# Layer 1 of a four-layer graph network in blocks of two chunks, with nine weight buffers, and three smaller edits in layer 3

## The chip, the cores and the metric

The kernel runs on one core of one Trainium2 chip. A core has five engines with a stream of instructions each: TensorE (PE in the profile; its weight loads are a row of their own, PEld), VectorE (DVE), ScalarE (ACT), GpSimd (POOL) and SyncE (SP), which issues most of the DMAs. The metric is the device time in microseconds (us) of one execution, given as the median of several runs. Lower is better.

## The reference, cut to what matters

Four layers, each of which ends in a residual sum and a layer norm. `x` is 2708 x 256, `adj` is 2708 x 2708, about 1.2% of it filled, with a full diagonal; all is float32.

```python
def layer1(x, adj, W, a, gamma, beta):          # attention with 4 heads of 64
    h = (x @ W).reshape(n, heads, head_dim)
    src = einsum('nhd,d->nh', h, a[:head_dim, 0])
    dst = einsum('nhd,d->nh', h, a[head_dim:, 0])
    e = src[:, :, None] + dst.T[None, :, :]
    e = where(e > 0, e, 0.2 * e)
    e = where(adj[:, None, :] > 0, e, -9e15)
    out = einsum('nhm,mhd->nhd', softmax(e, axis=-1), h).reshape(n, 256)
    return layernorm(out) * gamma + beta

def layer3(x, adj, neigh_W, lin_W):
    h = adj @ (x @ neigh_W.T) / (adj.sum(axis=1, keepdims=True) + 1.0)
    return concatenate([x, h], axis=-1) @ lin_W.T

x = layernorm(x + adj @ (x * W0))
x = layernorm(x + layer1(x, adj, ...))
x = layernorm(x + layer2(x, adj, ...))          # three heads of attention, two GRU cells
x = layernorm(x + layer3(x, adj, ...))
```

## The kernel before

**Tiles.** The 2708 rows make NT = 22 tiles of 128 rows (P), the last of 20. A tile of source rows is a "chunk" (c) where it is summed over. The four layers follow one another, with work of neighbouring layers drawn into one another where buffers allow. Each engine works through its own instructions in the order in which the program issued them, except that `tc.issue_after(instruction)` holds what stands under it until after that instruction in the order.

**Layer 1 (L780 to L858).** The destination rows are split into six groups of tiles (`spans`: 4, 4, 4, 4, 3, 3), worked in three pairs g = 0, 2, 4 of 1024, 1024 and 660 columns. Each pair takes two passes, q = 0 and 1, of two heads each: six passes over 22 chunks. The exponential of the leaky logits is split into factors that depend on one side only: `rise` belongs to the source row, `fall` to the destination. For each chunk and head of the pass DVE writes one tile p, 128 x 1024 (or 660), as max(fall, rise) x mask (L831, from a pool of five such tiles), where the fall tile `fall_b` holds the destination's factors in every partition. PE then does two things with the chunk's two p tiles. `heads` (L810 to L816) multiplies them with the 64 columns of `h` of each head into `acc`: four matmuls with weights 128x64 and 512 columns (330 in the last pair). `totals` (L818 to L825) sums them into `den`: four matmuls with weights 128x32. Both accumulate over all 22 chunks in PSUM (four buffers, tag `acc`), and ACT copies them out after the pass (L844, L852). The order is turned round with each chunk, T0 H0, H1 T1, T2 H2, H3 T3 and so on, if T and H are a chunk's totals and heads:

```python
for part in (heads, totals)[:: -1 if c % 2 == 0 else 1]:
    part(c, ps, dict(start=(c == 0), stop=(c == NT - 1)))
    if part is (totals, heads)[c % 2]:
        step(c)
```

`step(c)` issues one step of the work left over from the pair before: `layer1_end` (transposes L688 and L689, normalisation on ACT, DVE and POOL) in pass q = 0, `layer1_logits` (L750, L767) in pass q = 1.

**Fall tiles.** `fall_b` is [128, 4 heads, 1024], 16 KB in each partition, in two buffers. `load_fall` (L412) fills half of one by a DMA that gives one DRAM row to all partitions (`bcast_rows`, L106). The tiles of g = 0 and g = 2 are loaded on GpSimd's queue in layer 0, after its tiles 3, 7, 11 and 15; that of g = 4 on SP's queue at the start of the third pair (L784 to L786), once the first buffer is free.

**Layer 3.** `adj @ h` is done by seven products in place of eight: the destination columns come in three units of 430, 430 and 366 columns (`units3`), each over MH = 11 chunks. `seven` (L307) makes four sums of blocks on DVE (L313 to L316, out of the tile `p` that SP's queue loads, L273) and issues seven matmuls (L326). `gathered` (L330) adds the accumulators up at a unit's end (L337, L340, L343, L344); it returns its last add, and every chunk of the next unit, whichever it is, is issued with its sums behind it: `with tc.issue_after(summed.ins): seven(...)` (L1410). The first unit's sums stand behind the last gathering of layer 2, and in this unit the last steps of layer 2's node update (L1163 to L1233) are drawn in between the matmuls.

`rows3` and `row3` (L1365 to L1390) finish 128 rows at a time: PE transposes, DVE adds the residual (L1368), takes the moments (`bn_stats` L170, `bn_aggr` L172, an add L174), GpSimd takes the power -1/2 (L175). The row tile is closed by `flush()`, which is called after the next row tile's moments: DVE forms -mean x rs (L1361), ACT applies scale and bias (L1362), and a DMA stores the tile (L1363), on ACT's queue for odd tiles and on SP's for even ones. Two row tiles, 19 and 20 (`last3`), are not part of the units; they are summed directly at the end (L1428), with the rows of the last unit drawn in between, and tile 20 is the last to be closed.

Of the kernel before, what the change touches and what calls it, by code (L numbers as in the profile page):

```python
# [9 lines left out]
F32 = mybir.dt.float32  # L10
# [4 lines left out]
AF = mybir.ActivationFunctionType  # L15
ALU = mybir.AluOpType
# [3 lines left out]
P = 128  # L20
# [7 lines left out]
def kernel(  # L28
# [24 lines left out]
    nc = tc.nc  # L53
    N, F = x.shape
    NT = -(-N // P)
    FC = F // P
    HD = a1.shape[0] // 2
    H = F // HD
# [3 lines left out]
    W = GT * P  # L62
# [7 lines left out]
    spans = [(sum(sizes[:i]), sum(sizes[: i + 1])) for i in range(len(sizes))]  # L70
# [11 lines left out]
    last3 = [t for t in range(NT) if min(P, N - t * P) == P][-2:]  # L82
# [22 lines left out]

    def bcast_rows(d, lo, n):  # L106

        return bass.AP(tensor=d.tensor, offset=d.offset + lo, ap=[[0, P], [d.shape[1], d.shape[0]], [1, n]])

# [32 lines left out]
    fall_d = dram.tile([H, N], F32, name="fall_d")  # L142
# [249 lines left out]
    mask = mask_pool.tile([P, NT, MP], FP8, name="mask")  # L392
# [5 lines left out]
    if True:  # L398
# [6 lines left out]
        rise = keep.tile([P, NT, H], F32, name="rise")  # L405
# [5 lines left out]
        if True:  # L411
            def load_fall(dst, g, queue):  # L412
                at, w = spans[g][0] * P, width(*spans[g])
                off = at - spans[g - g % 2][0] * P
                queue.dma_start(dst[:, :, off : off + w], bcast_rows(fall_d, at, w))

            def layer1_projection(pool, t):
                n = sz(t)
# [23 lines left out]

                for g in [g for g, (lo, hi) in enumerate(spans[:4]) if hi == t + 1]:
                    load_fall(falls[g // 2], g, nc.gpsimd)

# [4 lines left out]
            with pool("l0", 2) as l0:  # L450
# [165 lines left out]
                fallp = fall_stack.enter_context(pool("fallp", 2, side="right"))  # L616
                falls = [fallp.tile([P, H, 2 * W], F32, tag="fall_b", name="fall_b") for _ in range(2)]
                nc.sync.dma_start(gamma_b, bcast(gamma, F))
# [36 lines left out]
            if True:  # L655
# [124 lines left out]
                for g in range(0, len(spans), 2):  # L780
                    segs = spans[g : g + 2]
                    at, w = segs[0][0] * P, width(segs[0][0], segs[-1][1])
                    if g >= 4:
                        falls.append(fallp.tile([P, H, 2 * W], F32, tag="fall_b", name="fall_b"))  # L784
                        for i in range(len(segs)):
                            load_fall(falls[-1], g + i, nc.sync)  # L786
                    cols = [(lo * P - at, width(lo, hi)) for lo, hi in segs]
# [18 lines left out]
                    for q in range(H // 2):  # L806
# [19 lines left out]

                        for c in range(NT):
                            ps = []
                            for i in range(2):
                                p = l1.tile([P, 2 * W], F32, tag="p", name="p", bufs=5)  # L830
                                nc.vector.scalar_tensor_tensor(  # L831
                                    p[:, :w], falls[g // 2][:, 2 * q + i, :w], rise[:, c, 2 * q + i : 2 * q + i + 1],
                                    mask[:, c, at : at + w], ALU.max, ALU.mult,
                                )
                                ps.append(p)

                            for part in (heads, totals)[:: -1 if c % 2 == 0 else 1]:
                                part(c, ps, dict(start=(c == 0), stop=(c == NT - 1)))
                                if part is (totals, heads)[c % 2]:
                                    step(c)  # L840
                        got = []
# [263 lines left out]
    with (  # L1105
# [250 lines left out]
        def flush():  # L1356

            while ended:
                t, o, mean, rs = ended.pop()
                n = sz(t)  # L1360
                nc.vector.scalar_tensor_tensor(mean, mean, -1.0, rs, ALU.mult, ALU.mult)  # L1361
                nc.scalar.activation(o[:n], o[:n], AF.Identity, scale=rs, bias=mean)  # L1362
                (nc.scalar if t % 2 else nc.sync).dma_start(out[t * P : t * P + n, :], o[:n])  # L1363
# [31 lines left out]
        for u, (_, w) in enumerate(units3):  # L1395
            m = accumulators()
            for i, c in enumerate(lead):
                early3 = u == 0 and max(ends_at[2 * c], ends_at[2 * c + 1]) + 1 < len(units)
                if u == 0:
                    if not early3:  # L1400
                        while urgent or later:
                            between()
                    hq[c] = quarter_sums(xqp, h3, c, "hq")
                pa = nright.tile([P, 2, 2, W], F32, tag="p", name="p", bufs=3)
                load_pairs(units3, u, c, pa, NH3, tiles3)
                if i == MH - 3:
                    o8 = hold.tile([P, 4 * W // F, F], F32, tag="blk", name="o8", bufs=2)
                    for j, t in enumerate(complete(u)):
                        nc.gpsimd.dma_start(o8[: sz(t), j], y3_d[t])
                with tc.issue_after(summed.ins):  # L1410
                    seven(nright, m, pa, h3, hq[c], c, w, i == 0, i == MH - 1, range(7) if early3 else (2, 5))
            y, summed = gathered(nleft, m, w, W, "yk")
            later.append(rows3(u, y, o8))
# [287 lines left out]
```

## Time and profile before

| | us |
|---|---|
| median of three runs | 1857.94 |
| the runs | 1857.53, 1857.94, 1859.26 |
| the profiled execution | 1858.13 |
| its span, first to last instruction | 1856.3 |
| PE busy in it | 1826.3 |
| DVE busy | 1279.9 |
| ACT busy | 700.2 |
| POOL busy | 272.3 |
| p tiles on DVE (L831), 264 of them | 293.8 busy, 30.0 idle before them |
| heads on PE (L813), 1056 records | 214.5 busy |
| totals on PE (L822), 1056 records | 114.9 busy |
| -mean x rs on DVE in layer 3 (L1361), 22 of them | 3.5 busy, 10.7 idle before them |

A row of the profile's groups names the line, the engine, the operation and the tiles (output <- inputs), how often it ran, how long it was busy, and how long its engine stood idle just before it, with what ended that idle time. In a timeline the first number is the start in us from the span's start and the second the length; x16 says that sixteen such records follow one another. An f32 matmul leaves two records. In a windows table each line is a stretch of time with the busy time and number of instructions (x) of each engine in it. The granted TensorE clock was 0.998 of full speed.

### The profile page before, as it was taken

The numbers are of one execution on the slowest core, as the hardware profiler recorded it, in microseconds if no ns is written. First come the engines' busy times: TensorE is split into PE (matmuls) and PEld (weight loads), VectorE is DVE, ScalarE is ACT, GpSimd is POOL, SyncE is SP. The second block draws the span as 40 slices with busy tenths as digits, with TensorE's granted clock in tenths as the row PEclk, the third lists the DMA queues.
The fourth block names the chain that finished last, engine by engine and source line by source line (L and its number), as shares of the span: only waits on it lengthen the run. The fifth ranks groups of instructions, "written<-read, shape, count | busy, mean of one in ns | idle before, by whom it ended". The sixth has DMA issues, their size and how long they took to land.

```text
span 1856.3 us, 23052 instructions
## 1 busy us (share of the span) xinstructions
PE 1826.3 (98%) x7512; PEld 1031.6 (56%) x7512; DVE 1279.9 (69%) x2263; ACT 700.2 (38%) x1444; POOL 272.3 (15%) x426
## 2 busy tenths in 40 slices
PE   9999999999999999999999999999999999999997
PEld 7788842233345886788444444444445556654555
DVE  5443479999898654654558887777887768844664
ACT  3544410023144203211555665555665546321011
POOL 1211220001012411000002000111200302111111
PEclk9999999999999999999999999999999999999999
DMA  8344410100002667764556665454554535634764
GB/s 299 134 148 148 161 41 1 30 1 7 18 7 73 146 145 191 170 145 116 171 143 203 181 175 164 120 169 113 163 156 110 148 100 139 164 106 118 199 166 122
DMA packets 435101, 237.32 MB, mean 128 GB/s; under 512 B 184363, under 2 KB 422348, under 8 KB 432540
## 3 DMA queue, kind: packets, MB, share of 16 engines
q1 hardware_dynamic: 422414, 208.66, 41.2%
q0 software_dynamic: 8208, 22.59, 3.8%
q10 hardware_dynamic: 4350, 4.50, 0.7%
q8 instruction: 62, 1.02, 0.2%
q14 instruction: 67, 0.55, 0.1%
HBM read 223.00 MB, written 12.66 MB: 127 GB/s over the span
## 4 chain that ended last, share of the span: by engine, by line
PE 85%; DMA 5%; DVE 4%; SPq 3%; issue 1%; ACT 1%; POOL 1%; POOLq 0%; DVEq 0%; ACTq 0%
PE m L326 40%; PE acc L813 11%; PE acc L213 8%; PE bank L1187 7%; PE den L822 6%; PE bank L1163 3%; SPq L273 2%; PE bank L1230 2%; PE gate L1062 2%; DMA strip<-in_adj_t_dram 2%; DMA p<-in_adj_t_dram 1%; PE pm L423 1%; PE pq L983 1%; PE m L1428 1%; DMA blk<-in_adj_t_dram 1%
## 5 line engine op out<-in xcount | busy, mean ns | idle before, releaser
L831 DVE SCALAR_TENSOR_TENSOR p<-fall_b,rise,mask 128x1024 f32<-128x1024 f32 (+1 forms) x264 | 293.8, 1156 | 30.0 <-PE den L822 14.7
L1328 ACT ACTIVATE p<-st,e_neg 128x1024 f32<-128x1024 f32 (+1 forms) x198 | 197.4, 1040 | 195.0 <-PE m L326 189.2
L326 PE MATMUL m<-s,xq 128*128 128x512 f32 (+3 forms) x660 | 230.1, 467 | 0.0
L813 PE MATMUL acc<-p,h 128*64 128x512 f32 (+2 forms) x1056 | 214.5, 548 | 0.0
L326 PE MATMUL m<-p,xq 128*128 128x512 f32 (+1 forms) x396 | 182.9, 544 | 0.1
L213 PE MATMUL acc<-turn,strip 128*128 128x257 f32 x792 | 181.8, 379 | 0.0
L1331 ACT ACTIVATE p<-p 128x1024 f32<-128x1024 f32 (+1 forms) x198 | 178.8, 942 | 0.2
L313 DVE TENSOR_TENSOR s<-p 128x512 f32<-128x512 f32 (+3 forms) x132 | 81.7, 619 | 137.6 <-PE m L326 114.4
L326 PE MATMUL m<-p,x 128*128 128x512 f32 (+1 forms) x396 | 167.7, 542 | 0.3 <-DVE supt L343 0.3
L1332 DVE TENSOR_TENSOR p<-p,blk 128x1024 f32<-128x1024 f32 (+1 forms) x132 | 143.0, 1103 | 35.7 <-ACT p L1331 25.7
L326 PEld LDWEIGHTS m<-s,xq 128*128 128x128 f32 x660 | 124.5, 190 | 76.1 <-issue 59.5
L213 PEld LDWEIGHTS acc<-turn,strip 128*128 128x128 f32 x792 | 147.2, 190 | 20.3
L813 PEld LDWEIGHTS acc<-p,h 128*64 128x64 f32 x1056 | 69.9, 136 | 136.7 <-issue 128.0
L326 PE MATMUL m<-s,x 128*128 128x512 f32 (+3 forms) x330 | 127.2, 467 | 0.0
L326 PEld LDWEIGHTS m<-p,xq 128*128 128x128 f32 x396 | 74.6, 190 | 76.9 <-issue 61.1
L326 PEld LDWEIGHTS m<-p,x 128*128 128x128 f32 x396 | 74.8, 190 | 75.5 <-issue 60.7
L822 PE MATMUL den<-p,h 128*32 128x512 f32 (+2 forms) x1056 | 114.9, 548 | 0.0
L468 ACT ACTIVATE below<-strip 128x384 bf16<-128x384 f32 x132 | 78.5, 594 | 69.8 <-DMA strip<-in_adj_t_dram 66.4
L284 POOL TENSOR_TENSOR blk<-blk,offdiag 128x128 f32<-128x128 f32 (+3 forms) x50 | 30.9, 622 | 367.4 <-DMA blk<-in_adj_t_dram 300.0
L326 PEld LDWEIGHTS m<-s,x 128*128 128x128 f32 x330 | 62.0, 190 | 39.2 <-issue 34.3
L314 DVE TENSOR_TENSOR p<-p 128x512 f32<-128x512 f32 (+3 forms) x132 | 82.0, 621 | 2.3
L316 DVE TENSOR_TENSOR s<-p,s 128x512 f32<-128x512 f32 (+3 forms) x132 | 81.1, 615 | 1.9
(285 smaller groups left out, 2586.5 us busy)
## 6 DMA issues: line engine op xcount, KB each, us to landing
strip<-in_adj_t_dram SPq DMA_DIRECT2D x19, 1408.0 KB, 6.3
blk<-in_adj_t_dram SPq DMA_DIRECT2D x88, 256.0 KB, 3.4
blk<-in_adj_t_dram SPq DMA_DIRECT2D x88, 192.0 KB, 4.1
pa<-in_adj_t_dram SPq DMA_DIRECT2D x110, 128.0 KB, 2.6
turn<-in_adj_t_dram SPq DMA_DIRECT2D x44, 256.0 KB, 3.1
blk<-in_adj_t_dram SPq DMA_DIRECT2D x88, 128.0 KB, 2.5
p<-in_adj_t_dram SPq DMA_DIRECT2D x88, 128.0 KB, 2.7
turn<-in_adj_t_dram SPq DMA_DIRECT2D x44, 192.0 KB, 3.2
```

What stands on the lines that cost most here:

```text
L213: at = nc.tensor.matmul(acc, s[:, c, :n], rhs(c), start=(c == 0), stop=(c == NT - 1))
L313: nc.vector.tensor_tensor(s1, a21, a22, ALU.add)
L314: nc.vector.tensor_tensor(a21, a21, a11, ALU.subtract)
L316: nc.vector.tensor_tensor(s4, a12, s2, ALU.subtract)
L326: nc.tensor.matmul(dst[:, :w], lt, rt, start=start and not (one_bank and i in (3, 4, 6)), stop=stop and not (one_bank and i in (1, 2, 5)))
L813: nc.tensor.matmul(acc[s][i * HD : (i + 1) * HD, :ws], hs[c][:, 2 * q + i, :HD], ps[i][:, p0 : p0 + ws], **flags,)
L822: nc.tensor.matmul(den[j : j + CT, :ws], hs[c][:, 2 * q + i, HD + 1 - CT :], ps[i][:, p0 : p0 + ws], **flags,)
L831: nc.vector.scalar_tensor_tensor(p[:, :w], falls[g // 2][:, 2 * q + i, :w], rise[:, c, 2 * q + i : 2 * q + i + 1], mask[:, c, at : at + w] ...
L1187: nc.tensor.matmul(g[:, :w], lt, rt, start=(q == 0), stop=(q == len(terms) - 1))
L1328: nc.scalar.activation(p[:, :, :w], st_k[:, :, :w], AF.Relu, scale=-1.0, bias=e_neg[:, at, k : k + 1])
L1331: nc.scalar.activation(p[:, :, :w], p[:, :, :w], AF.Exp, scale=-1.0)
L1332: nc.vector.tensor_tensor(p[:, :, :w], p[:, :, :w], blk[:, i, :, :w], ALU.mult)
```

## The change

1. In layer 1 the chunks are taken in blocks of two. All four p tiles of a block are issued first, then one part for both chunks, then the other for both; the order of the parts is turned round with each block: T0 T1 H0 H1, H2 H3 T2 T3, T4 T5 H4 H5. The pool of p tiles has nine buffers instead of five (16 KB more in a partition). `step` is called once after each part.
2. A fall tile holds the two heads of one pass, [128, 2, 1024], in two buffers (16 KB less in a partition). The two of g = 0 are loaded on GpSimd's queue in layer 0, after its tiles 3 and 7, two DMAs each time; the other four on SP's queue, each after the p tiles of a pass of the pair before, two DMAs each.
3. In `flush()` -mean x rs is formed on GpSimd instead of DVE. For the very last tile (20) one DVE operation, (x - mean) x rs, stands in for both the product and ACT's activation.
4. The first chunk of each unit of layer 3 is not issued behind the gathering's last add.

PE's instructions are the same in kind and number. DVE has 22 small operations (128x1, one of them 20x1) less and one of 128x256 more, ACT one of 128x256 less, GpSimd 21 of 128x1 more.

```diff
@@ -103,9 +103,9 @@
                 yield t, a, b
             lo -= sz(t)
 
-    def bcast_rows(d, lo, n):
-
-        return bass.AP(tensor=d.tensor, offset=d.offset + lo, ap=[[0, P], [d.shape[1], d.shape[0]], [1, n]])
+    def bcast_rows(d, row, rows, lo, n):
+
+        return bass.AP(tensor=d.tensor, offset=d.offset + row * d.shape[1] + lo, ap=[[0, P], [d.shape[1], rows], [1, n]])
 
     def pool(name, bufs=1, **kw):
         return tc.tile_pool(name=name, bufs=bufs, reuse_waits="tile", **kw)
@@ -409,10 +409,10 @@
         ps_t = ps_t_stack.enter_context(pool("ps_t", 4, space=PSUM, side="right"))
         ps_acc = acc_stack.enter_context(pool("ps_acc", 4, space=PSUM))
         if True:
-            def load_fall(dst, g, queue):
+            def load_fall(dst, g, q, queue):
                 at, w = spans[g][0] * P, width(*spans[g])
                 off = at - spans[g - g % 2][0] * P
-                queue.dma_start(dst[:, :, off : off + w], bcast_rows(fall_d, at, w))
+                queue.dma_start(dst[:, :, off : off + w], bcast_rows(fall_d, 2 * q, 2, at, w))
 
             def layer1_projection(pool, t):
                 n = sz(t)
@@ -440,8 +440,9 @@
                 nc.scalar.copy(turned[:, :n], pf[:H, 0, :n])
                 nc.gpsimd.dma_start(fall_d[:, t * P : t * P + n], turned[:, :n])
 
-                for g in [g for g, (lo, hi) in enumerate(spans[:4]) if hi == t + 1]:
-                    load_fall(falls[g // 2], g, nc.gpsimd)
+                for g in [g for g, (lo, hi) in enumerate(spans[:2]) if hi == t + 1]:
+                    for q, dst in enumerate(falls):
+                        load_fall(dst, g, q, nc.gpsimd)
 
             w0_b = keep.tile([P, F], F32, name="w0_b")
             quarter = keep.tile([P, CT], F32, name="quarter")
@@ -614,7 +615,7 @@
                 gamma_b = keepr.tile([P, F], F32, name="gamma_b")
                 beta_b = keepr.tile([P, F], F32, name="beta_b")
                 fallp = fall_stack.enter_context(pool("fallp", 2, side="right"))
-                falls = [fallp.tile([P, H, 2 * W], F32, tag="fall_b", name="fall_b") for _ in range(2)]
+                falls = [fallp.tile([P, 2, 2 * W], F32, tag="fall_b", name="fall_b") for _ in range(H // 2)]
                 nc.sync.dma_start(gamma_b, bcast(gamma, F))
                 nc.sync.dma_start(beta_b, bcast(beta, F))
                 layer0_scale(ahead, last)
@@ -780,10 +781,6 @@
                 for g in range(0, len(spans), 2):
                     segs = spans[g : g + 2]
                     at, w = segs[0][0] * P, width(segs[0][0], segs[-1][1])
-                    if g >= 4:
-                        falls.append(fallp.tile([P, H, 2 * W], F32, tag="fall_b", name="fall_b"))
-                        for i in range(len(segs)):
-                            load_fall(falls[-1], g + i, nc.sync)
                     cols = [(lo * P - at, width(lo, hi)) for lo, hi in segs]
                     cut = min(cols[1][0], (w // 2 + P // 4) // (P // 2) * (P // 2))
                     halves_at = [(0, cut), (cut, w - cut)]
@@ -824,20 +821,28 @@
                                         ps[i][:, p0 : p0 + ws], **flags,
                                     )
 
-                        for c in range(NT):
-                            ps = []
-                            for i in range(2):
-                                p = l1.tile([P, 2 * W], F32, tag="p", name="p", bufs=5)
-                                nc.vector.scalar_tensor_tensor(
-                                    p[:, :w], falls[g // 2][:, 2 * q + i, :w], rise[:, c, 2 * q + i : 2 * q + i + 1],
-                                    mask[:, c, at : at + w], ALU.max, ALU.mult,
-                                )
-                                ps.append(p)
-
-                            for part in (heads, totals)[:: -1 if c % 2 == 0 else 1]:
-                                part(c, ps, dict(start=(c == 0), stop=(c == NT - 1)))
-                                if part is (totals, heads)[c % 2]:
-                                    step(c)
+                        fall_b = falls.pop(0)
+                        for b, c0 in enumerate(range(0, NT, 2)):
+                            block = {}
+                            for c in range(c0, min(c0 + 2, NT)):
+                                block[c] = []
+                                for i in range(2):
+                                    p = l1.tile([P, 2 * W], F32, tag="p", name="p", bufs=9)
+                                    nc.vector.scalar_tensor_tensor(
+                                        p[:, :w], fall_b[:, i, :w], rise[:, c, 2 * q + i : 2 * q + i + 1],
+                                        mask[:, c, at : at + w], ALU.max, ALU.mult,
+                                    )
+                                    block[c].append(p)
+
+                            for i, part in enumerate((heads, totals)[:: -1 if b % 2 == 0 else 1]):
+                                for c, ps in block.items():
+                                    part(c, ps, dict(start=(c == 0), stop=(c == NT - 1)))
+                                if c0 + i < NT:
+                                    step(c0 + i)
+                        if g + 2 < len(spans):
+                            falls.append(fallp.tile([P, 2, 2 * W], F32, tag="fall_b", name="fall_b"))
+                            for i in range(len(spans[g + 2 : g + 4])):
+                                load_fall(falls[-1], g + 2 + i, q, nc.sync)
                         got = []
                         for s, (p0, ws) in enumerate(cols):
                             sb = keepr.tile([P, W], F32, tag=f"sum{q}{s}", name=f"sum{q}{s}")
@@ -1358,8 +1363,11 @@
             while ended:
                 t, o, mean, rs = ended.pop()
                 n = sz(t)
-                nc.vector.scalar_tensor_tensor(mean, mean, -1.0, rs, ALU.mult, ALU.mult)
-                nc.scalar.activation(o[:n], o[:n], AF.Identity, scale=rs, bias=mean)
+                if t == last3[-1]:
+                    nc.vector.tensor_scalar(o[:n], o[:n], mean, rs, ALU.subtract, ALU.mult)
+                else:
+                    nc.gpsimd.tensor_scalar(mean, mean, rs, -1.0, ALU.mult, ALU.mult)
+                    nc.scalar.activation(o[:n], o[:n], AF.Identity, scale=rs, bias=mean)
                 (nc.scalar if t % 2 else nc.sync).dma_start(out[t * P : t * P + n, :], o[:n])
 
         def row3(t, o, acc):
@@ -1407,7 +1415,7 @@
                     o8 = hold.tile([P, 4 * W // F, F], F32, tag="blk", name="o8", bufs=2)
                     for j, t in enumerate(complete(u)):
                         nc.gpsimd.dma_start(o8[: sz(t), j], y3_d[t])
-                with tc.issue_after(summed.ins):
+                with tc.issue_after(summed.ins) if i else nullcontext():
                     seven(nright, m, pa, h3, hq[c], c, w, i == 0, i == MH - 1, range(7) if early3 else (2, 5))
             y, summed = gathered(nleft, m, w, W, "yk")
             later.append(rows3(u, y, o8))
```

More of the change, by code (lines that the diff above doesn't have):

```diff
@@ L1 @@
 import itertools
-from contextlib import ExitStack
+from contextlib import ExitStack, nullcontext
 import concourse.bass as bass
```

## The prediction

> **What bounds the kernel now.** I read the page's busy shares first, then the chain of waits, then each stage that the change touches: the six passes of layer 1 as windows, one pass as a timeline of PE and of DVE, and the timeline of the end of layer 3.
>
> ```profile
> PE 1826.3 (98%) x7512; PEld 1031.6 (56%) x7512; DVE 1279.9 (69%) x2263; ACT 700.2 (38%) x1444; POOL 272.3 (15%) x426
> PE 85%; DMA 5%; DVE 4%; SPq 3%; issue 1%; ACT 1%; POOL 1%; POOLq 0%; DVEq 0%; ACTq 0%
> ```
>
> PE is busy nearly always and holds 85% of the chain that ended last, so a gain must either shorten PE's own stream or remove one of the 30 us (1856.3 - 1826.3) in which PE does nothing. The windows below are the six passes of layer 1, in order.
>
> ```profile
> core 0: us, PE busy (x) PEld busy (x) DVE busy (x) ACT busy (x) POOL busy (x), PEclk, DMA share, GB/s
> 247.50:309.00 61.50, 61.50 (x366) 17.20 (x369) 57.05 (x55) 2.06 (x8) 8.21 (x6) 1.00 0.04 10
> 309.00:368.80 59.80, 59.80 (x360) 16.23 (x356) 54.57 (x44) 2.33 (x4) 0.00 (x0) 1.00 0.04 11
> 368.80:431.90 63.10, 63.10 (x384) 18.86 (x380) 60.68 (x85) 26.28 (x129) 8.44 (x7) 1.00 0.04 13
> 431.90:498.00 66.10, 66.10 (x408) 21.80 (x404) 53.88 (x48) 9.20 (x25) 6.34 (x9) 1.00 0.06 17
> 498.00:541.60 43.60, 43.60 (x388) 19.30 (x380) 41.64 (x76) 22.63 (x117) 5.91 (x5) 1.00 0.00 1
> 541.60:587.90 46.30, 46.30 (x401) 22.12 (x394) 38.82 (x60) 12.42 (x37) 11.03 (x20) 1.00 0.08 23
> ```
>
> PE's busy time equals the window in every pass: 340.4 us without a gap. DVE, which makes the p tiles, is busy 306.6 us and comes second, closest in passes 3 and 5 (60.7 of 63.1, 41.6 of 43.6). PE's timeline in pass 2:
>
> ```profile
> 318.93 1.92 PE L822 MATMUL den<-p,h 128*32 128x512 f32 x16
> 320.79 3.65 PE L813 MATMUL acc<-p,h 128*64 128x512 f32 x16
> 324.37 1.92 PE L822 MATMUL den<-p,h 128*32 128x512 f32 x16
> 326.23 3.65 PE L813 MATMUL acc<-p,h 128*64 128x512 f32 x16
> ```
>
> Two chunks' totals (T) start every 5.44 us. An f32 matmul leaves two records, heads (H, 64 columns) run two abreast and totals (32 columns) four abreast, so two chunks of H take 8 slots and two of T take 4. Weight loads inside one H stand 0.43 us apart (0.4285). Eight slots are 3.43 us, but H lasts 3.58 (324.37 - 320.79); four are 1.71, but T lasts 1.86. Each change between the two shapes thus costs 0.15 us. The check on all six passes: 12 x 0.4285 x 11 = 56.6 us for a pass of 1024 columns and 36.8 for one of 660, about 2.6 of transposes in passes 1, 3 and 5, some 5.2 of logits in passes 4 and 6, and the changes of shape counted in PE's order, 26, 22, 26, 30, 26, 30 = 160, give 61.8, 59.8, 63.0, 66.2, 43.3, 46.3: the measured lengths within 0.3 us. So nothing but PE's stream sets layer 1.
>
> The end of the kernel (timeline, all engines):
>
> ```profile
> 1839.97 4.48 PE L1428 MATMUL m<-turn,p 128*128 128x256 f32 x20
> ...
> 1844.60 0.16 DVE L1361 SCALAR_TENSOR_TENSOR bn_mv<-bn_mv,bn_rs 128x1 f32<-128x1 f32 x1 [0.72 <-POOL bn_rs L175]
> ...
> 1846.70 0.15 DVE L1361 SCALAR_TENSOR_TENSOR bn_mv<-bn_mv,bn_rs 20x1 f32<-20x1 f32 x1 [0.72 <-POOL bn_rs L175]
> 1846.78 0.47 DVE L1368 SCALAR_TENSOR_TENSOR y<-m,rdeg,y 128x256 f32<-128x256 f32 x1
> ...
> 1848.84 0.16 DVE L1361 SCALAR_TENSOR_TENSOR bn_mv<-bn_mv,bn_rs 128x1 f32<-128x1 f32 x1 [0.72 <-POOL bn_rs L175]
> 1849.03 0.60 ACT L1362 ACTIVATE y<-y,bn_mv,bn_rs 128x256 f32<-128x256 f32 x1 [1.54 <-DVE bn_mv L1361]
> 1849.65 0.33 SPq L1363 DMA_DIRECT2D out_dram<-y  x1
> ```
>
> PE's last matmul ends at 1844.45, yet its row starts on DVE at 1846.78. DVE stands 0.72 us before each L1361 for GpSimd's power (L175), a row takes it 2.15 us (start to start of L1368), and a backlog has built up.
>
> [...] 0.15 us a change, none between matmuls of one shape. [...] for 128x1 the trace's nearest row is L175, 0.54 us alone at the end, and I use that.
>
> **Part 1, blocks of two chunks.** T0 T1 | H0 H1 H2 H3 | T2 T3 T4 T5 | H4...: one change of shape per block instead of one per chunk. Counting changes in PE's new order, which is known without running it (first pass not quite regular, transposes included), gives 24, 12, 18, 22, 19, 22 = 117. 43 fewer x 0.149 us = -6.4 us. PE's instructions are the same.
>
> What this needs from DVE: four p's before each block, out of nine buffers instead of five. In pass 2 DVE makes a p each 1.24 us, 54.6 a pass; with the other vector work that its new order puts into each pass I get 60.5 us against a PE pass of 63.1 - 1.2 = 61.9 for pass 3, 41.4 against 43.6 - 1.0 = 42.6 for pass 5 and 42.2 against 46.3 - 1.2 = 45.1 for pass 6. It keeps up, but by about 1 us, with three p's of lead as the only store. Bounds: nothing, or up to 2 us of stalls over both passes. I take +0.4. At pass boundaries the denominators are done four matmul groups earlier, so their copies on ACT free the buffer that the next pass's first H needs within T0 T1 (1.86 us); at layer 1's end the 0.85 us of acc copies come after the last H, +0.15 to 0.3, inside the same allowance.
>
> **Part 2, fall tiles by half.** Four DMAs in layer 0 stay four on GpSimd's queue with half the bytes; the second and third pairs add eight on SP where two stood. They stand on SP between the loads of layer 0 and those of layer 2, whose first begins at 588; SP's issue of one takes 0.37 us and waits only for the last DVE read of the pass before. They land 5.6 to 7.1 us after issue in the trace and are read a whole pass (some 60 us) later. 0 us; they would cost only if landing took longer than a pass.
>
> **Part 3, mean times scale on GpSimd.** Per row DVE loses a 128x1 operation (0.16) and, above all, the wait: 0.47 + 0.43 + 0.18 + 0.15 with their gaps is 1.35 us, less than the 1.5 us in which PE delivers rows. The backlog goes, and the last row starts at about 1844.65: -2.13 us. For the last tile, one DVE operation of 128x256 (0.42, from the row of L170, up to 0.5) replaces 0.16 and 0.60 with their handover: 1848.84 to 1849.26 instead of 1849.63, -0.37. From SP's issue to the end the 6.65 us stay. Sum -2.5 (bounds -2.7 to -2.0). GpSimd gets 21 operations of about 0.55; its queue carries a power each 1.5 us at the end, so 1.1 of 1.5 is used, and the power of the last row stands ahead of nothing that is unfinished. The earlier rows' outputs leave later by half a us and are not last.
>
> **Part 4, first chunk's sums not behind the gathering.** Each unit of layer 3 starts with sums (L313 to L316) held behind the last add of the gathering (L344). For unit 0 PE stands 2.75 us between the two first chunk's stretches:
>
> ```profile
> 1609.99 0.60 DVE L313 TENSOR_TENSOR s<-p 128x430 f32<-128x430 f32 x1
> 1610.35 0.99 PE L326 MATMUL m<-p,turn 128*128 128x430 f32 x2 [1.03 <-DMA p<-in_adj_t_dram]
> 1613.78 0.99 PE L326 MATMUL m<-p,turn 128*128 128x430 f32 x2 [1.72 <-DMA p<-in_adj_t_dram]
> ```
>
> In the new order L313 to L315 stand before the gathering's first add (L337, 1606.88 now). Their data is issued from 1599.6 and lands at about 1606.6 to 1607, so the gathering ends about 2 us later (1.8 us of sums less the idle time before it), while PE has its sums sooner: I take 2.0 us of stall for 2.75. In units 1 and 2 the sums fit in DVE's idle time before the gathering (6.3 and 5.0 us) and stalls of 0.37 and 0.80 shrink by half. In all -0.75 - 0.2 = about -0.9, bounds -2.5 to +3.
>
> Sum: -6.4 + 0.4 - 2.5 - 0.9 = -9.4 us. The profiled execution, span 1856.3 and 1.8 around it, 1858.1 us, becomes 1848.7. It is 0.2 above the median of the runs (1857.94), so the forecast is 1848.6 us.
>
> **The rivals.**
> - B: DVE becomes the bound. For: passes 3 and 5 have 2 us to spare now, and PE wants to be faster by 1.2 each; a lead of two blocks must also be built up at each start. Against: DVE's waits in layer 1 (14.7 us behind totals, 13.8 behind heads) are all for PE. Layer 1 then gains 2.5 us: 1848.6 + 3.9 = 1852.5.
> - C: the data of the first chunk's sums comes too late in all units, the gathering waits behind them and PE with it, with no gain and 1.3 us of new stall at each of the three (2 us of delay, 0.7 of it covered by PE's next matmuls): 1848.6 + 0.9 + 3 x 1.3 = 1853.4. Against: SP has issued those loads 7 us before in unit 0.
> - D, the slower side: the matmuls of layer 3's unit 0 hide the node update of the last group of columns. In the new PE order two or three fewer of them stand before each half-step's transposes (L1220). From the last gate matmul (1681.00) to those transposes (1684.16) is 3.16 us, four times; each of seven tiles then waits 0.57 for its copy. All uncovered: 12.6 + 4.0 = 16.6 us, 1865.2. It decides from 13.1 us on, that is only when nearly all of it is uncovered; PE stands still for 0.6 us between 1615 and 1720 now.
> - E: the change of shape costs what it did, because the 0.15 belongs to each first matmul of a chunk and not to the change. Then only parts 3 and 4 are left: 1855. The pass check, with its transposes, speaks against it.
>
> **How the numbers follow.** Forecast 0.62, B 0.17, C 0.12, D 0.05, E 0.04. Bounds of the forecast's own costs: 1845.5 (stalls nothing, first chunk -2.5) to 1851.0. The range reaches to B and C and leaves out D and E: 1845.5 to 1853.5. About 0.2%, 3.7 us, can be told from no change: faster is below 1854.2, which the forecast, B and three quarters of C give, 0.88; within 0.2%, 0.07; slower, 0.05.
>
> **What would show it.** Passes of 61.2, 58.3, 61.9, 64.9, 42.6 and 45.1 us, each shorter than now by the changes of shape that it loses (2, 10, 8, 8, 7, 8) times 0.149; den and acc groups of 32 records; DVE's idle in them still for PE. At the end no wait of DVE for GpSimd but the last, and the last row starting 0.2 us after PE's last matmul. In unit 0 one stall of PE of about 2 us. The prediction fails if PE waits for p in layer 1, or if PE's stalls grow between 1600 and 1700.

## The result, and the profile after

The changed kernel takes 1853.53 us (median of seven runs, 1850.31 to 1855.39) beside 1859.17 (1857.53 to 1859.54) of the kernel before: a ratio of 0.9967, interval 0.9957 to 0.9976. On the base of the prediction that is 1857.94 x 0.9967 = 1851.8 us, inside the range of 1845.5 to 1853.5 and 3.2 us above the forecast of 1848.6; the bare median lies on the range's upper edge. Of the 9.4 us forecast, about two thirds came. The profiled execution took 1851.74 us with a span of 1850.0, 6.3 less than before. The page of the changed kernel, busy shares and the chain of waits:

```profile
PE 1821.8 (98%) x7512; PEld 1038.5 (56%) x7512; DVE 1273.9 (69%) x2242; ACT 699.1 (38%) x1443; POOL 273.0 (15%) x447
PE 91%; DMA 3%; DVE 2%; ACT 1%; SPq 1%; issue 1%; POOL 0%; POOLq 0%; DVEq 0%; ACTq 0%
```

PE is still the engine that counts. To see where the 6.3 us come from, I cut both spans, which are given to 0.1 us, at PE's own events:

| stretch | before | after | difference |
|---|---|---|---|
| start to layer 1's first totals | 247.49 | 246.77 | -0.7 |
| to layer 2's first matmul | 343.75 | 340.93 | -2.8 |
| to layer 3's first matmul | 1016.48 | 1016.32 | -0.2 |
| to PE's last matmul | 236.73 | 235.47 | -1.3 |
| to the end of the span | 11.85 | 10.51 | -1.3 |

The first row is no effect of the change: over the thirteen profiles of this study it lies anywhere between 246.8 and 252.8. So runs are compared below by these stretches. Layer 1 repeats to about 0.1 us; layer 3 doesn't: in the four kernels that leave part 4 out (before, and blocks, tail and split of the experiments) it takes 235.7 to 237.5 us. The six passes of layer 1 in the changed kernel, as windows:

```profile
core 0: us, PE busy (x) PEld busy (x) DVE busy (x) ACT busy (x) POOL busy (x), PEclk, DMA share, GB/s
246.80:308.70 61.90, 61.90 (x362) 17.56 (x361) 59.24 (x59) 2.64 (x9) 4.94 (x6) 1.00 0.09 26
308.70:367.10 58.40, 58.40 (x354) 17.21 (x352) 53.16 (x46) 2.33 (x4) 0.00 (x0) 1.00 0.06 19
367.10:429.00 61.90, 61.90 (x378) 19.55 (x376) 59.68 (x83) 25.79 (x126) 8.22 (x6) 1.00 0.03 12
429.00:494.10 65.10, 65.10 (x402) 22.47 (x401) 54.04 (x54) 9.79 (x26) 7.22 (x10) 1.00 0.10 28
494.10:536.30 42.20, 42.20 (x377) 21.12 (x376) 38.59 (x70) 19.99 (x110) 4.72 (x4) 1.00 0.00 1
536.30:585.00 48.70, 47.16 (x402) 24.27 (x401) 36.02 (x59) 14.70 (x45) 11.01 (x20) 0.96 0.07 20
```

Passes 2 to 5 have come out at 58.4, 61.9, 65.1 and 42.2 us, within 0.4 us of the numbers predicted. Pass 6 has not: 48.7 for 45.1, longer than before. It is the only one in which PE is not busy throughout (47.16 of 48.70) and in which the granted clock (the column behind POOL, 0.96) is below 1. (Its window ends with the last logits matmuls, 0.9 us, which come after the last heads here and before the last totals in the kernel before.) Its timeline, all engines:

```profile
554.62 3.35 DVE L831 SCALAR_TENSOR_TENSOR p<-fall_b,rise,mask 128x660 f32<-128x660 f32 x4
...
555.38 0.19 ACT L666 ACTIVATION_READ_ACCUMULATOR turn<-turn,o_mean 128x1 f32 x1
557.88 0.16 DVE L674 TENSOR_SCALAR o_var<-o_var 128x2 f32<-128x2 f32 x1
...
557.96 0.66 PE L751 MATMUL tr<-ident,x 128*128 128x128 f32 x4
558.19 1.23 POOL L675 TENSOR_TENSOR o_rs<-o_var,neg_half 128x2 f32<-128x2 f32 x1 [7.55 <-DVE o_var L674]
558.54 1.35 PE L819 MATMUL den<-p,h 128*32 128x320 f32 x16
...
559.46 0.48 ACT L738 ACTIVATE o_mean<-o_mean,o_rs 128x1 f32<-128x1 f32 x2 [3.89 <-POOL o_rs L675]
...
559.84 1.08 ACT L739 ACTIVATE x<-turn,o_mean,o_rs 128x256 f32<-128x256 f32 x2
560.83 0.56 ACT L753 COPY turn<-tr 128x512 f32<-128x512 f32 x1
...
561.44 1.05 PE L768 MATMUL pm<-uw,turn 128*128 128x3 f32 x8 [1.54 <-ACT turn L753]
...
563.71 6.35 PE L810 MATMUL acc<-p,h 128*64 128x384 f32 x32
```

Read from the bottom: PE stands 1.54 us before a logits matmul (L768) for ScalarE's copy of the transposed tile (L753). ScalarE's queue has L738 ahead of this copy, another pair's scaling, which waits for GpSimd's power (L675), and that for VectorE's variance (L674). Its data is there at 555.57 (ScalarE's last step), but it stands in VectorE's queue behind the block's four p tiles (554.62 to 557.97) and starts 2.3 us late. And PE has only one part, 1.28 us of totals, between the transposes (L751) and the matmul that needs the copy. Then the heads from 563.71 on take 6.28 us to the next group, where 32 such records take 4.59 elsewhere. Windows of this stretch:

```profile
core 0: us, PE busy (x) PEld busy (x) DVE busy (x) ACT busy (x) POOL busy (x), PEclk, DMA share, GB/s
560.35:563.76 3.41, 2.32 (x26) 1.49 (x27) 2.97 (x6) 2.28 (x9) 1.39 (x2) 1.00 0.17 54
563.76:567.17 3.41, 3.41 (x14) 1.42 (x14) 0.98 (x2) 0.43 (x2) 0.00 (x0) 0.50 0.08 23
567.17:570.60 3.43, 3.43 (x33) 1.65 (x33) 2.49 (x4) 0.33 (x2) 1.23 (x1) 1.00 0.02 5
```

For 3.41 us PE was granted half its clock (0.50): 14 records, where the window after has 33. At 0.50 that is some 1.7 us lost, an estimate (half of 3.41), on top of the wait of 1.54 us. In late_pm and both, below, PE doesn't wait there and the clock stays full in layer 1.

At the start of layer 3's unit 0 (timeline of the changed kernel) PE again stands, for 2.20 us, and then runs at half clock, 1608.24 to 1611.65 (0.50 granted, 6 records, where the 3.41 us behind have 12):

```profile
1605.70 0.60 DVE L315 TENSOR_TENSOR s<-s,p 128x430 f32<-128x430 f32 x1
1606.22 0.83 DVE L337 TENSOR_TENSOR yk<-m1s,m 128x660 f32<-128x660 f32 x1
...
1607.11 0.99 PE L326 MATMUL m<-p,turn 128*128 128x430 f32 x2 [2.20 <-DVE yk L337]
```

The second matmul of the first chunk writes the accumulator that the gathering's first add (L337) has to read, and this add now stands behind three sums. The end of the changed kernel:

```profile
1839.54 0.48 DVE L1376 SCALAR_TENSOR_TENSOR y<-m,rdeg,y 128x256 f32<-128x256 f32 x1 [2.95 <-PE m L1436]
...
1841.69 0.41 DVE L1367 TENSOR_SCALAR y<-y,bn_mv,bn_rs 128x256 f32<-128x256 f32 x1 [0.74 <-POOL bn_rs L175]
1842.13 0.33 SPq L1371 DMA_DIRECT2D out_dram<-y  x1
```

The backlog is gone: the last row starts 0.05 us after PE's last matmul (1839.49), and the last store is issued 2.64 us after it instead of 5.20. But from the store to the end it is 7.87 us instead of 6.65. GpSimd's drain, one of the closing steps of the program, is in the way. Before, then after, from the view of the last line's instructions (shortest, middle and longest in ns, first and last start):

```profile
L1697 POOLq DRAIN  x3: 50/107/4801, 1849.4 to 1856.1; - x3
```

```profile
L1705 POOLq DRAIN  x3: 46/106/4478, 1844.6 to 1849.7; - x3
```

Before, the drain of 4.8 us began 0.25 us ahead of the last store's issue. After, it begins 2.5 us behind it (the store had landed at 1844.40).

### The profile page after: what moved, and what is told of

It reads as the page before. It is cut to its first block, busy times and chain, and to the rows that moved or that the text cites. A ratio compares the mean times of both kernels' runs of the same rounds, so it can differ in the third digit from the quotient of the medians.

```text
span 1850.0 us, 23081 instructions
## 1 busy us (share of the span) xinstructions
PE 1821.8 (98%) x7512; PEld 1038.5 (56%) x7512; DVE 1273.9 (69%) x2242; ACT 699.1 (38%) x1443; POOL 273.0 (15%) x447
## 4 chain that ended last, share of the span: by engine, by line
PE 91%; DMA 3%; DVE 2%; ACT 1%; SPq 1%; issue 1%; POOL 0%; POOLq 0%; DVEq 0%; ACTq 0%
PE m L326 44%; PE acc L810 11%; PE acc L213 8%; PE bank L1192 7%; PE den L819 6%; PE gate L1067 4%; PE bank L1168 3%; PE bank L1235 2%; DMA strip<-in_adj_t_dram 2%; PE m L1436 1%; SPq L273 1%; PE pm L423 1%; PE pq L988 1%; ACT below L469 1%; PE pm L768 0%
## 5 line engine op out<-in xcount | busy, mean ns | idle before, releaser
L831 DVE SCALAR_TENSOR_TENSOR p<-fall_b,rise,mask 128x1024 f32<-128x1024 f32 (+1 forms) x264 | 288.0, 1152 | 25.7 <-PE den L819 15.6
L326 PEld LDWEIGHTS m<-s,xq 128*128 128x128 f32 x660 | 124.5, 190 | 76.1 <-issue 59.7
```

Of the source, the lines that this page charges most:

```text
L326: nc.tensor.matmul(dst[:, :w], lt, rt, start=start and not (one_bank and i in (3, 4, 6)), stop=stop and not (one_bank and i in (1, 2, 5)))
L831: nc.vector.scalar_tensor_tensor(p[:, :w], fall_b[:, i, :w], rise[:, c, 2 * q + i : 2 * q + i + 1], mask[:, c, at : at + w], ALU.max, ALU. ...
```

## The experiments

The parts one by one, each in the kernel before, then repairs of the changed kernel. "Layer 1" is from its first totals to its last heads or totals, "layer 3" from its first matmul to PE's last, "end" from there to the end of the span, all of the profiled execution; the ratio is to runs of the kernel before that were taken beside each group of runs (medians 1857.76, 1858.47 and 1859.41), so ratios can be compared between groups, medians less well. Where chunks come in blocks, up to 0.9 us of logits matmuls come after this end of layer 1; old_order and split have them inside it like the kernel before.

| kernel | layer 1 | layer 3 | end | median | ratio, interval |
|---|---|---|---|---|---|
| before | 340.41 | 236.73 | 11.85 | | |
| after | 337.39 | 235.47 | 10.51 | 1853.53 | 0.9967, 0.9957 to 0.9976 |
| blocks (parts 1, 2) | 337.41 | 235.73 | 12.56 | 1856.60 | 0.9990, 0.9983 to 0.9996 |
| tail (part 3) | 340.41 | 236.20 | 8.66 | 1855.62 | 0.9988, 0.9979 to 0.9997 |
| first (part 4) | 340.42 | 237.28 | 11.90 | 1857.80 | 0.9998, 0.9990 to 1.0006 |
| split (part 2) | 340.42 | 237.50 | 12.52 | 1858.52, one run | |
| old_order | 340.42 | 233.47 | 10.21 | 1854.64 | 0.9985, 0.9973 to 0.9996 |
| var_pool | 338.83 | 235.51 | 10.12 | 1852.68 | 0.9973, 0.9962 to 0.9984 |
| late_pm | 334.39 | 235.99 | 10.33 | 1849.39 | 0.9945, 0.9928 to 0.9962 |
| second | 337.29 | 233.19 | 10.10 | 1850.32 | 0.9958, 0.9948 to 0.9967 |
| shift2 | 337.34 | 236.05 | 10.10 | 1853.08 | 0.9966, 0.9956 to 0.9975 |
| both | 334.39 | 234.72 | 10.24 | 1848.49 | 0.9943, 0.9929 to 0.9957 |
| triple | 338.49 | 233.54 | 10.26 | 1853.32 | 0.9968, 0.9957 to 0.9979 |

**blocks**: the changed kernel's layer 1, with `flush` and the hold on the first chunk as before.

> The kernel before with parts 1 and 2 of the change alone (blocks, nine buffers, fall tiles by half). Theory A: in the changed kernel passes 2 to 5 of layer 1 came out as predicted (58.4, 61.9, 65.1, 42.2 us) and pass 6 did not (48.7 instead of 45.1), because PE waited 1.5 us for ScalarE's copy of the transposed tile before a logits matmul and then ran 3.4 us at half clock. The same pass should show the same wait here, layer 1 about 338 us long, and the kernel 2 to 3.5 us faster than before, some 1856. Rival: the wait in pass 6 belongs to the whole changed kernel's run and not to the blocks; then layer 1 is about 334.5 us and the kernel 6 us faster. Layer 3 as in the kernel before under both.

Layer 1 is that of the changed kernel to 0.02 us, with the same wait of PE (1.55 us for L753) and half clock after it (567.2 to 570.6). The loss belongs to the blocks. The whole time fell by 0.10%, 1.9 us, a little under the 2 to 3.5 expected: the end is longer than before by 0.7 us, which neither theory had foreseen (see split).

**tail**: `flush` alone.

> The kernel before with part 3 alone (mean times scale on GpSimd, last tile closed by one VectorE operation). Theory A: the last row starts within 0.2 us of PE's last matmul, as in the changed kernel, but the closing steps of the engines after the last store take longer, so that the stretch from PE's last matmul to the end falls from 11.85 us to about 10.5: 1.3 us faster. Rival, the prediction: 2.5 us faster, a stretch of 9.35 us. PE's stream up to its last matmul unchanged under both.

Both were too small: the end fell by 3.2 us. The row and the store behave as in the changed kernel, but here GpSimd's drain begins at 1849.5, 0.1 us after the last store's issue. So part 3 by itself shortens the end by more than predicted, and something else takes 1.9 us of it away in the changed kernel.

**first**: the hold on the first chunk alone.

> The kernel before with part 4 alone (the first chunk's sums of each unit of layer 3 not behind the gathering). Theory A: at the start of unit 0 PE waits once, about 2.2 us, for the accumulator that the gathering's first add (L337) reads late, and then runs at half clock for about 3.4 us; in spite of it PE is through unit 0 some 1.5 us earlier; units 1 and 2 change by under 0.3 us; 1 to 1.5 us faster in all. Rival: without a stretch at half clock unit 0 gains 3 us, and the kernel is 3 us faster.

PE waits once, 2.24 us for L337, and half clock follows (1613.1 to 1616.5). Up to the last gate matmul unit 0 is 1.56 us shorter, as theory A has it, but the next two units took 2 us longer in this execution (one sum came 1.1 us late). In the whole time nothing can be seen: 0.9998, with an interval of 1.9 us faster to 1.1 slower.

**var_pool**: the changed kernel with the variance of the layer-1 normalisation on GpSimd.

```diff
-                        nc.vector.tensor_scalar(v, v, 1.0 / F, EPS, ALU.mult, ALU.add)
+                        nc.gpsimd.tensor_scalar(v, v, 1.0 / F, EPS, ALU.mult, ALU.add)
```

> The changed kernel with one operation of the layer-1 normalisation (variance/256 + eps, 128x2, 22 of them) on GpSimd instead of VectorE. Theory A: in the changed kernel that operation stands behind four p tiles in VectorE's queue, GpSimd's power, ScalarE's scaling and the copy behind it come late, and PE stands still before a logits matmul. Without it in VectorE's queue the wait in pass 6 goes and with it the stretch at half clock: pass 6 of 45 to 45.5 us instead of 48.7, the kernel about 3 us faster than the changed one, 1850. Rival: the lateness comes from elsewhere (VectorE's other operations of that chain, or the clock falls without a wait); pass 6 stays over 47 us and the time near 1853.5.

The wait in pass 6 fell from 1.54 to 0.28 us and the half clock there is gone: theory A held for the cause of that wait. But the order that the scheduler found for ScalarE has changed at the start of pass 4 (timeline):

```profile
433.02 0.48 ACT L738 ACTIVATE o_mean<-o_mean,o_rs 128x1 f32<-128x1 f32 x2 [1.04 <-POOL o_rs L675]
433.41 1.08 ACT L739 ACTIVATE x<-turn,o_mean,o_rs 128x256 f32<-128x256 f32 x2
434.51 1.07 ACT L849 COPY sum<-acc 128x512 f32<-128x512 f32 x2
435.15 5.35 PE L810 MATMUL acc<-p,h 128*64 128x512 f32 x16 [2.04 <-ACT sum L849]
```

The same scaling, still waiting for GpSimd, now stands ahead of the copy that frees an accumulator, PE waits 2.04 us, and half clock follows there. Layer 1 is 1.4 us longer than in the changed kernel: a miss as a repair.

**late_pm**: only PE's order changes; one more step lies between a pair's transposes and its logits matmuls.

```diff
                     yield
+                    if late:
+                        yield
 
                     pm = ps_t.tile([P, 4, P], F32, tag="tr", name="pm")
```

> The changed kernel with one more step between the transposes of a pair's logits and their matmuls, so that PE has a part more of other work between them; the order on VectorE, ScalarE and SyncE stays as it is. Theory A: PE's wait of 1.54 us in pass 6 for ScalarE's copy is covered, the stretch at half clock behind it (3.4 us, 1.7 lost) does not come, and layer 1 from its first totals to its last heads takes 334 us instead of 337.4; the kernel about 3 us faster than the changed one. Rival: the lateness moves on as it did with the variance on GpSimd, PE waits at another place of layer 1, and it stays over 336.5 us.

As theory A has it: layer 1 takes 334.39 us, 3.0 less than in the changed kernel, and the clock stays full in it. In PE's timeline of pass 6 two parts (2.49 us here) lie between transposes and matmul, without a wait:

```profile
562.09 0.66 PE L751 MATMUL tr<-ident,x 128*128 128x128 f32 x4
562.67 2.49 PE L821 MATMUL den<-p,h 128*32 128x320 f32 x32
565.10 1.05 PE L770 MATMUL pm<-uw,turn 128*128 128x3 f32 x8
```

**old_order**: the changed kernel with the loop of the kernel before, chunk by chunk, and nine buffers.

> The changed kernel with the order of heads and totals of the kernel before (turned round with each chunk, p tiles issued chunk by chunk), but with the nine buffers and the fall tiles by half. Theory A: the gain of passes 2 to 5 comes from fewer changes between the two shapes alone; the passes are as before, 59.8, 63.1, 66.1 and 43.6 us. Rival: part of it comes from the deeper store of p tiles; they are shorter than before by 0.5 us or more each.

Layer 1 is 340.42 us, that of the kernel before to 0.01. So the gain of the blocks comes from the order alone, and the count of changes of shape gives its size; nine buffers without blocks bring nothing.

**second**: the first chunk's sums held behind the gathering's second add.

```diff
-                with tc.issue_after(summed.ins) if i else nullcontext():
+                with tc.issue_after((summed if i else early[-1]).ins):
```

(`early` collects that add in `gathered`.)

> The changed kernel with the first chunk's sums of each unit of layer 3 held behind the gathering's second add (L340) instead of not at all. VectorE's order at the start of unit 0 becomes L337, L340, a sum, L343, a sum, L344, a sum. Theory A: PE's wait of 2.2 us there was for L337, which stood behind three sums; now it is under 0.7 us, no stretch at half clock follows, and unit 0 from its first matmul to the last gate matmul takes 69 us instead of 71.7. Rival: the wait belongs to the load of p, which has just landed, and stays over 1.5 us with the half clock after it; unit 0 over 71 us.

PE's wait is 1.10 us, now for the load of p, and no half clock follows:

```profile
1604.37 0.84 DVE L339 TENSOR_TENSOR yk<-m1s,m 128x660 f32<-128x660 f32 x1 [3.50 <-PE m L326]
...
1607.92 0.96 PE L326 MATMUL m<-p,turn 128*128 128x430 f32 x2 [1.10 <-DMA p<-in_adj_t_dram]
```

Up to the last gate matmul it is 70.8 us, between the two expectations; for layer 3 as a whole 233.19 instead of 235.47. The wait for L337 came from the sums ahead of it, and the load of p is what comes next. In the whole time the two kernels' intervals overlap (0.9958 and 0.9967).

**shift2**: two more DMAs on SyncE's queue in layer 0.

> The changed kernel with two more DMAs on SyncE's queue in layer 0 (gamma and beta loaded in two halves each). The last store then uses the DMA counter that it uses with part 3 alone. Theory A: at the end GpSimd waited for the last store to land because of the counter that this store was given, before its closing drain of 4.5 us; with the counters turned by two it does not wait, and the stretch from PE's last matmul to the end is 8.7 us instead of 10.5. Rival: the wait comes from GpSimd's own instructions (it loads fewer tiles and forms more products); the stretch stays at 10 to 10.6 us. Everything before as in the changed kernel.

The end stays at 10.10 us and GpSimd's drain begins 2.2 us behind the store's issue: theory A fell. **split** then takes part 2 alone:

> The kernel before with part 2 alone: fall tiles by half, the four later ones loaded on SyncE's queue; order, five buffers and the rest as before. In all kernels with parts 1 and 2 GpSimd stands at the end until the last store has landed (about 2.3 us after its issue) before a drain of 4.48 us; in the three without them it does not and drains for 4.80 us. Theory A: this goes with part 2, since GpSimd's loads change: GpSimd waits here too, the drain is 4.48 us, the stretch from PE's last matmul to the end 12.5 us instead of 11.85. Rival: it goes with the nine buffers; then the stretch is 11.85 us and the drain 4.80. Layer 1 as before, 340.4 us.

```profile
L1699 POOLq DRAIN  x3: 50/106/4474, 1851.4 to 1856.5; - x3
```

The last store was issued at 1849.39: GpSimd waits 2.0 us before its drain, and the end is 12.52 us, as theory A has it. So the later drain comes with the fall tiles by half, not with the blocks, the buffers or part 3. The expectation that GpSimd waits until the store has landed is not borne out: here the drain begins 0.85 us before the landing, at 1852.27, and in blocks and var_pool 0.6 and 0.5 us before it. By which dependence GpSimd has to wait there is left open; that it is the counter of the last store, as shift2 supposed, is not borne out.

**both** (late_pm and second together) and **triple** (both, with blocks of three chunks):

> The changed kernel with the extra step before the logits' matmuls and with the first chunk's sums held behind the gathering's second add. Theory A: both waits of PE and both stretches at half clock are gone; layer 1 takes 334.4 us from its first totals to its last heads, layer 3 from its first matmul to PE's last 233 us instead of 235.5; the granted clock stays full from layer 1 to PE's last matmul; about 1848 us, 5 less than the changed kernel. Rival: the gains do not add up, since the second falls into a stretch that then waits for the load of p; 1849.5 or more.

Layer 1 came out as expected to 0.01 us, and from there to PE's last matmul the clock stayed full. In unit 0 PE waited 1.67 us for the load of p, so layer 3 gained only 0.75 us over the changed kernel in this execution. With a median of 1848.49 it is the fastest of all, 0.9943 of the kernel before; from late_pm (0.9945) it can't be told apart.

> The kernel of the run both with blocks of three chunks instead of two, with the nine buffers. It has about 18 fewer changes between the two shapes of matmul, 2.7 us at 0.149 each, but only three p tiles of lead where six are needed for a block. Theory A: VectorE keeps up but for small stalls, layer 1 takes 332 to 333.5 us instead of 334.4. Rival: PE waits for p tiles in each block whose totals come last; layer 1 takes over 335 us.

The rival held: layer 1 takes 338.49 us. In triple's list of waits PE's weight loads wait for p tiles:

```profile
PEld den L823 <- DVE p L835: 14.7, 19, 1.5
```

That is 14.7 us in 19 waits (part of it beside running matmuls), where the run both has 3.9 in ten. Six tiles for a block and three of lead are too few; more than nine buffers were not tried.

## Why the prediction was right or wrong, point by point

**The total: in the range, in part by luck.** The range was drawn to reach rivals B and C. Layer 1 fell about as far short as B has it, but through a wait that neither the forecast nor a rival names.

**The price of a change of shape: right.** 0.149 us a change gave passes 2 to 5 within 0.4 us, and old_order shows that nothing but the order brings a gain in part 1. Long groups of 32 records (3.64 and 7.09 us in the timeline of pass 1) show the same:

```profile
291.00 3.64 PE L819 MATMUL den<-p,h 128*32 128x512 f32 x32
294.57 7.09 PE L810 MATMUL acc<-p,h 128*64 128x512 f32 x32
301.59 3.64 PE L819 MATMUL den<-p,h 128*32 128x512 f32 x32
```

3.57 us from one start to the next for eight slots of totals is 8 x 0.4285 + 0.14.

**"What this needs from DVE ... I take +0.4": this step failed.** It weighed VectorE's work against PE's by pass and allowed 0 to 2 us. The sums erred on the safe side (60.5, 41.4 and 42.2 us for passes 3, 5 and 6, where the windows have 59.7, 38.6 and 36.0), VectorE is not the bound in them, and rival B fell. But a sum over a pass doesn't show the order in the queue. Four p tiles in a row delay each small operation behind them by up to 3.4 us, and the chain VectorE, GpSimd, ScalarE, PE of the pair before has one place, in pass 6, where PE has 1.28 us of other work and no more. The wait cost 1.54 us and the half clock, by the estimate above, some 1.7; of these 3.2 us late_pm gets 3.0 back. Most of the rest of layer 1's shortfall is pass 1, 61.9 us for 61.2, whose groups are broken up: PE's records change shape 30 times in it, where 24 were counted; in the kernel before it is 28 for the 26 counted. The four more make 0.6 us at 0.149 each, an estimate. Layer 1 gave 2.8 us, close to the 2.5 of rival B, at another place and for another reason.

**Part 2 at 0 us: wrong at a place that wasn't looked at.** The loads themselves cost nothing in layer 1, but GpSimd's drain at the end of the program starts about 2 us later with them (split, blocks): 0.7 us in the kernel before, and 1.9 together with part 3, whose faster end makes the drain the last thing.

**Part 3, -2.5 us: the mechanism right, the size wrong in the sum.** The backlog, the start of the last row, the single operation in place of two are as predicted: 2.56 us earlier from PE's last matmul to the store. "From SP's issue to the end the 6.65 us stay" was the wrong term: it is 7.87 us in the changed kernel and 6.0 in tail. That tail and the changed kernel differ in this is the drain. The product on GpSimd takes 0.27 us (L1369), half of what was assumed.

**Part 4, -0.9 us: a gain in unit 0, for a stall of another kind; in the whole not shown.** From layer 3's first matmul to the last gate matmul it is 73.3 to 73.6 us in the four kernels without part 4 and 71.5 to 71.8 in five with it (after, first, var_pool, late_pm, shift2): some 1.7 us less. The 1.3 us of layer 3 as a whole are no more than executions differ there, and first shows no gain in the whole time. The remaining stall is 2.2 us, close to the 2.0 taken, but it is a wait for L337, and the half clock behind it (3.41 us at 0.50) takes away some 1.7 us by the same estimate. In second and old_order, where PE waits 1.1 and 1.3 us there and the clock stays full in layer 3, it takes 233.2 and 233.5 us, the shortest of all. Rival C named the late gathering; the three boundaries didn't behave alike: in the later units the changed kernel's PE waits 0.23 us in all, where it waited 1.2 before.

**Rivals D and E fell**: PE's filling in unit 0 was enough, the gates show no new wait of weight, and passes 2 to 5 followed the count of changes.

**Sums that don't come out of their terms.** Pass 1 with 2.6 us of transposes and 26 changes gives 63.1 us, not 61.8; it has 14 records that are neither heads nor totals where pass 3 has 32. The range's ends are not the bounds of its terms either: the least costs give some 1846.4, not 1845.5, and a first chunk at +3 us with 2 us of stalls gives over 1854, not 1851.0. And rival B's 1852.5 counts the forecast's own +0.4 twice. The forecast itself rests on none of these.

## What to carry to other kernels

Where an engine's instructions are put into larger groups to spare another engine, look not only at the sums but at what small operation now stands behind a whole group in the same queue (here L674, 2.3 us late behind four p tiles), and follow its chain to the engine that bounds; one more step of distance on PE, without any work less, was worth 3 us here. On the engine that bounds, look at the granted clock behind each wait: the waits of 1.54 to 1.56 us in pass 6 were followed by half clock, some 1.7 us more by the estimate above, and those of 1.49 to 1.57 us in layer 2 were not. And a last step that is made faster can leave another closing step in its place: here the store is issued 2.56 us sooner after PE's last matmul and the end is 1.3 us shorter, so the end of a program is to be read as a race of all engines.

## What the runs showed of the hardware that was not expected

The length of a wait alone does not tell whether half clock follows. It followed the wait of 1.54 to 1.56 us in pass 6 in all four kernels that have it (after, blocks, shift2, second), the wait of 1.9 to 2.3 us for L337 in all five (after, first, var_pool, late_pm, shift2), the one of 2.04 us in pass 4 of var_pool and, in split, waits of 0.94 and 0.34 us at the start of layer 2. It did not follow waits of 1.0 to 1.72 us at the start of unit 0 in before, blocks, old_order, second, both, triple and split, nor one of 2.04 us there in tail, nor one of 1.49 to 1.57 us in layer 2, near 1535 us, that all thirteen profiles have.

What decides, the runs do not show. In the changed kernel the 3.41 us ahead of the half clock in pass 6 have 2.32 us of busy PE (560.35 to 563.76, above; about 1 us of it are the eight matmuls of three columns), those ahead of the half clock in unit 0 have 1.21 (the first line). Tail's two waits, 0.99 and 2.04 us, lie in two stretches of this length, one behind the other, with 1.71 and 2.13 us (the second and third lines; full clock after both); the one ahead of first's half clock has 1.17 (the fourth line). The columns are those of the windows above:

```profile
1604.83:1608.24 3.41, 1.21 (x4) 0.68 (x4) 3.38 (x6) 0.00 (x0) 0.00 (x0) 1.00 1.12 260
1612.19:1615.61 3.42, 1.71 (x4) 0.68 (x4) 3.42 (x6) 0.00 (x0) 0.00 (x0) 1.00 1.10 254
1615.61:1619.02 3.41, 2.13 (x7) 1.44 (x8) 0.35 (x1) 0.00 (x0) 0.00 (x0) 1.00 0.34 88
1609.70:1613.11 3.41, 1.17 (x4) 0.49 (x3) 3.30 (x6) 0.00 (x0) 0.00 (x0) 1.00 1.17 270
```

In split some 2.1 us of busy PE stand ahead of the half clock that begins near 592.6, an estimate: 3.41 less the waits of 0.94 and 0.34. So PE's busy time ahead doesn't part the cases by itself: half clock came after 2.1 and 2.32 us and not after 1.71 and 2.13. No run was made that moves a wait, or other work beside it, to try this.

A stretch at half clock in layer 0, at about 51 to 57 us of the span, stands in five of the thirteen profiles (blocks, tail, late_pm, shift2, both; in both from about 51.8 to 55.2). At some 1.7 us each, by the estimate above, such stretches would be part of the spread of the whole times; that was not shown.

GpSimd's last drain takes 4.8 us in before, tail and first and 4.48 in the kernels with the fall tiles by half; it ends 0.8 to 2.2 us before the span does.
